# Resident convolution weights, other PSUM banks and an earlier start of the scan inputs in a two-layer attention, Mamba and mixture-of-experts kernel

## The chip, the cores and the metric

The kernel runs on one core of a Trainium2 chip. The core has five engines with an instruction queue each, which run in parallel and meet at semaphores: PE (TensorE, matrix products and transposes, into the eight banks of PSUM), DVE (VectorE), ACT (ScalarE, functions through tables that have to be loaded), POOL (GpSimd) and SP, which here only issues DMAs. Every engine works through its own queue in order: an instruction that waits holds back all that stand behind it. The metric is the time of one execution on the device in microseconds (us); less is better.

## The reference

Everything is float32, for 4 sequences (batches) of 1024 tokens with 128 features. Two layers, each with a mixer and a mixture of experts; shift, scale and gate of each come from a small product with a condition vector:

```python
h = _layernorm(x) * (1 + ca) + sa;  x = x + ga * _L0_attn_ref(h, Wq, Wk, Wv, Wo)
h = _layernorm(x) * (1 + cb) + sb;  x = x + gb * _L0_ffn_ref(h, gate_w, w1, w2)
h = _layernorm(x) * (1 + ca) + sa;  x = x + ga * _L1_attn_ref(h, W_in, conv_w, ...)   # layer 1's own mod
h = _layernorm(x) * (1 + cb) + sb;  x = x + gb * _L1_ffn_ref(h, router_w, w1, w2, bias)
```

- Attention of layer 0: 16 query heads of 64, 4 key/value heads, rotary embedding, causal softmax.
- Experts of layer 0: 8 experts with a hidden width of 176; each token goes to its two best by softmax, `silu(g) * u @ w2`.
- The mixer of layer 1 is a Mamba selective scan: `x, z = split(x @ W_in)`; a causal convolution over 4 tokens and silu; from its result B, C (16 states each) and `delta = softplus(...)`; then `h = exp(delta * A) * h + delta * B * u`, `y = sum(h * C)` over 1024 tokens for 128 x 16 states, plus `u * D`, times `silu(z)`, times `W_out`.
- Experts of layer 1: 8 experts of width 512 with a capacity of 512 tokens each, gelu, the two best of each token; tokens over the capacity are dropped.

## The kernel before, in words

The kernel is written with tiles and pools. A scheduler puts each engine's instructions in order by priority and dependencies, so the order of an engine follows the program only loosely; by hand are only the pairs of matmuls that are kept next to each other (`next_to`, line 197) and a few transfers that are issued after others. A pool's memory is given to later tiles when it is closed, and these wait for the last reader.

**Start.** The condition products run and the first features are normed. SP's queue then issues, in order: the attention weights (`wq` first, line 481 onwards), 44 DMAs that fill the slots of the experts in HBM with zeros (line 491), and the DMAs `rot_v` that swap halves for the rotary embedding (lines 508 and 509). `gate_wT` is loaded from ACT's queue.

**Attention.** Stages (b, c): a batch and a half of its heads. Each stage takes eight blocks of queries in the order 7, 0, 6, 1, 5, 2, 4, 3; `probabilities` makes the scores (`sc`, PE), the masked row extremes (DVE), the exponential (ACT) and the division (POOL); `turned` transposes them, `weighted` multiplies by v, `attend` by `wo`. Beside it run the layer-0 experts of the batch before: `sort_tokens` (line 331) finds each token's place and scatters rows to HBM (`blocks_in`), `Blocks` (lines 393 to 455) runs 23 blocks of 128 rows each (`turn` transposes three blocks, `first` makes `pf`, `second` the result `fye`), and `first_returns` (line 311) gathers the results (`fy`, POOL) and adds them to x (DVE, line 278). Batch 3's experts don't fit in and run beside the scans.

**Scans.** For each batch, `scan_inputs` (line 840) makes from the normed x the convolution (four products of `hT` with `conv_in`, into `p`), xc and sz (Silu on ACT), delta (`pd`, and the softplus in small steps on DVE with Exp on ACT), `dg` (DVE), dt, du (POOL, line 882), and bb and cc. Then come 16 steps m (NCH is 16), 8 for either half of the tokens, each with two of the 16 channel groups. A step is `scan` (line 898): two matmuls `pu` (PE, a bank each), two products with bb (DVE, line 911), two `da` (ACT), two scans `h` (DVE, line 915) and two products `hc` (POOL, line 919). `collected` gathers four hc into the bank `py`, `scan_output` multiplies by sz and W_out (`pw`) and adds to x. That makes 16 pairs and 32 scans for each batch, 64 pairs in all, numbered here by scans from 0 to 127.

Beside the steps run generators, written in the loop at lines 1189 to 1254. `Beside(steps, at, n)` means: from step m = at, n steps of the generator after each m, and the rest after the batch. In the list `beside` they are taken in order after each m, in `among` also between the scan and its gathers. Before the change: in batch 0 `first_returns(2)`, `sort_tokens(3)`, `shift_and_scale`; in batch 1 `first_blocks(3)`; in batch 2 `first_returns(3)`; in each, `dispatch` of the batch before (line 941: the norm, the routing and 16 scatters `slots_in`), and, last in the list, the `scan_inputs` of the next batch from m = 2 (5 in batch 2).

**The end.** `dispatch_last`, 16 calls of `expert` with 512 rows, `last_experts` for the last tokens in blocks of 128, and `collect`, which gathers and stores.

PSUM in layer 1, eight banks: `pu0` to `pu3` for the scans, `py`, `g` for the blocks, `m` for the inputs and the sort, `d` for dispatch, `pw` and every second block.

Of the kernel before, what the change touches and what calls it, by code (L numbers as in the profile page):

```python
# [18 lines left out]
P = 128  # L19
# [5 lines left out]
NEG = -1e30  # L25
LN_EPS = 1e-5
NE = 8
# [22 lines left out]
def adaln_two_layers(ctx: ExitStack, tc: tile.TileContext, I: dict, out: bass.AP):  # L50
# [11 lines left out]
    def load(pool, name, eng=nc.sync):  # L62
# [10 lines left out]
    causal = cst.tile([P, P], F32, name="causal")  # L73
    nc.gpsimd.memset(causal, 0.0)
    nc.gpsimd.affine_select(
        out=causal, in_=causal, compare_op=ALU.is_ge, fill=NEG, base=0, pattern=[[-1, P]], channel_multiplier=1
    )
# [127 lines left out]
    def top2_steps(logits, pool):  # L205
# [5 lines left out]
        def t2(tag):  # L211
            return pool.tile([P, TB], F32, tag=f"r_{tag}", name=f"r_{tag}")[:, :nt]

        def t3(tag):
            return pool.tile([P, TB, NE], F32, tag=f"r_{tag}", name=f"r_{tag}")[:, :nt]
# [43 lines left out]
    f_gate = load(keep, "gate_wT", nc.scalar)  # L259
    loads = []  # L260
# [70 lines left out]
    def sort_tokens(b, kept, pool, ps, tag, xtag="fxn"):  # L331
# [5 lines left out]
        yield from feature_steps(xn, hT, ps, modT[0][:, 4, b : b + 1], modT[0][:, 3, b : b + 1])  # L337
        pl = ps.tile([P, TB, NE], F32, tag="m", name="fpl")
# [8 lines left out]
        pin = ps.tile([P, TB + 1, NE], F32, tag="m", name="fpin")  # L347
# [45 lines left out]
    class Blocks:  # L393
# [9 lines left out]
        def load(self, n):  # L403
            rows_in = f_in[self.b].rearrange("(q p) d -> p q d", p=P)
            m = min(3, NB - 3 * n)
            self.xe = self.pool.tile([P, 3, D], F32, tag="fxe", name="fxe")
            nc.sync.dma_start(self.xe[:, :m], rows_in[:, 3 * n : 3 * n + m])
# [54 lines left out]
    QG = 32  # L462
    with ExitStack() as es:
# [19 lines left out]
        for j in range(4):  # L483
            rows = slice(j * QG, (j + 1) * QG)
            nc.gpsimd.tensor_copy(mask[rows, MW - QG :], causal[rows, rows])

# [174 lines left out]
        for at, (b, c) in enumerate(stages):  # L661
# [7 lines left out]
            back = first_returns(b - 2, ab, 3) if c == 1 and b > 1 else iter(())  # L669
# [45 lines left out]
    m_in = load(w1l, "m_in")  # L715
    m_cb = load(w1l, "m_cb")
    m_B = load(w1l, "m_B")
    m_C = load(w1l, "m_C")
    m_dt = load(w1l, "m_dt")
# [17 lines left out]
    with ExitStack() as es:  # L737
# [12 lines left out]
        conv_in = mc.tile([P, 4, D], F32, name="conv_in")  # L750
        nc.sync.dma_start(conv_in.rearrange("p k d -> p (k d)"), I["m_cwT"].to_broadcast([P, 4 * D]))
        nc.vector.tensor_mul(conv_in, conv_in, m_in[:, :D].unsqueeze(1).to_broadcast([P, 4, D]))

# [20 lines left out]
        def first_blocks(b):  # L774

            blocks = Blocks(b, fb, (ps_g, "g"), [(ps_g, "g"), (ps_m, "d")], rest)
# [63 lines left out]
        def scan_inputs(b):  # L840
# [12 lines left out]
            for tok in halves():  # L853
# [5 lines left out]
                mm(nc, p2, m_in[:, D:], hT[:, tok.start + 3 : tok.stop + 3])  # L859
# [38 lines left out]
        def scan(pair, g, carry, dt, du, bb, cc):  # L898
# [4 lines left out]
            for _ in pair:  # L903
                pus.append(ps_u.tile([P, 512], F32, tag=f"pu{next(turn) % 4}", name="pu"))
            for n in range(2):
# [3 lines left out]
                next_to(n == 0, lambda: mm(nc, pus[n], lhsT, du[rows, tok]))  # L909
# [187 lines left out]
        def last_experts():  # L1097
# [16 lines left out]
            def hidden(j):  # L1114
# [13 lines left out]
                ph = [ps_u.tile([P, NFC, P], F32, tag=f"pu{(j + r) % 4}", name="gph") for r in range(n)]  # L1128
# [59 lines left out]
        output = None  # L1188
        for b in range(B):
            sz, xc, *scanned = inputs.rest()  # L1190
            carry = mb.tile([P, NCH], F32, tag="carry", name="carry")
            beside, among = [], []
            if b == 0:
                beside.append(Beside(first_returns(B - 2, db, 6), 4, 1))
                beside.append(Beside(sort_tokens(B - 1, kept, db, ps_m, "hT2", "hx"), 2, 4))
                beside.append(Beside(shift_and_scale(), NCH - 3, 1))
            if b == 1:
                among.append(Beside(first_blocks(B - 1), 1, 1))
            if b == 2:
                beside.append(Beside(first_returns(B - 1, db, 6), 0, 2))  # L1200
            if sending is not None:
                beside.append(sending)
            if b + 1 < B:
                inputs = Beside(scan_inputs(b + 1), 5 if b == 2 else 2, 3 if b == 2 else 2)
                beside.append(inputs)
            hcs, late = [], None
            for m in range(NCH):
# [22 lines left out]
                if n == NCH // 2 - 1:  # L1230
# [5 lines left out]
                    hcs = []  # L1236
# [180 lines left out]
```

## Time and profile before

| | us |
|---|---|
| median of 3 runs | 2197.03 |
| the three runs | 2189.51, 2197.03, 2200.22 |
| the profiled execution | 2186.78 |
| its span | 2185.1 |
| first scores of attention | 93.44 |
| last `pw` of attention ends | 1424.7 |
| first `pu` | 1470.87 |
| scans of batches 0, 1, 2, 3 | 1471 to 1556, 1588 to 1686, 1686 to 1816, 1851 to 1934 |

The times in a profile count from the start of the span. The page gives each engine's busy time, and the granted clock of TensorE in 40 slices (9 is full). A line of a timeline has the start and the duration in us, the engine, the line of the kernel, the operation, output<-inputs, shapes, the count (on PE an fp32 matmul is more than one record), and in brackets the idle time before it and what released it. SPq and ACTq are DMA issues on those queues. A row of the table by stage has the stretch, its length, the busy time of PE, of PE's weight loads, DVE, ACT and POOL with their counts, the granted clock, and the DMA share and rate.

### The profile page before, as it was taken

How to read it: one execution, taken by the hardware profiler on the slowest of the kernel's cores; microseconds unless marked ns; L12 is line 12 of the kernel's file. 1: busy time of each engine (PE TensorE's matmuls, PEld its weight loads, DVE VectorE, ACT ScalarE, POOL GpSimd, SP SyncE). 2: the span in 40 equal slices, each digit the busy share in tenths (PEclk: the TensorE clock that was granted, in tenths of full speed). 3: DMA queues.
4: the chain of work that ended last, by engine and by line, in shares of the span. 5: the costliest groups of instructions: out<-in, count | busy, mean ns of one | idle time of the engine just before them, and what ended most of it. 6: DMA issues, size and time to landing. Idle time of an engine off the chain costs nothing. (4 is left out here: it accounts for less than half of the span.)

```text
span 2185.1 us, 29044 instructions
## 1 busy us (share of the span) xinstructions
PE 1832.8 (84%) x8957; PEld 972.7 (45%) x8957; DVE 1321.1 (60%) x4001; ACT 939.5 (43%) x2067; POOL 993.6 (45%) x1277
## 2 busy tenths in 40 slices
PE   5399999998999898999988999959698858859784
PEld 3144444454555354455444456523245423227563
DVE  5446566565667755667675566537587785861323
ACT  1145454653454464445374455433564334323221
POOL 1334444346333736523644633244563666571524
PEclk9699999999999998999999999965687757559897
DMA  6300101002222101222200212110121220012425
GB/s 224 126 1 20 30 1 38 12 19 55 72 64 76 48 1 44 77 66 64 77 6 29 69 58 75 35 34 0 35 71 51 75 99 20 1 51 82 131 72 153
DMA packets 103756, 123.59 MB, mean 57 GB/s; under 512 B 15024, under 2 KB 68656, under 8 KB 103600
## 3 DMA queue, kind: packets, MB, share of 16 engines
q1 hardware_dynamic: 84256, 99.01, 15.4%
q0 software_dynamic: 8192, 16.74, 2.5%
q10 hardware_dynamic: 11152, 5.97, 0.9%
q8 instruction: 71, 1.16, 0.2%
q14 instruction: 85, 0.70, 0.1%
HBM read 67.85 MB, written 32.90 MB: 46 GB/s over the span
## 5 line engine op out<-in xcount | busy, mean ns | idle before, releaser
L586 POOL TENSOR_SCALAR pr<-pr,den 128x32 f32<-128x32 f32 (+31 forms) x512 | 353.2, 705 | 301.9 <-DVE den L583 295.8
L580 ACT ACTIVATE pr<-pr,nb 128x32 f32<-128x32 f32 (+31 forms) x512 | 371.6, 727 | 196.9 <-DVE nb L567 193.6
L595 PE MATMUL pt<-ident,pr 128*128 128x128 f32 x2304 | 341.9, 283 | 47.6 <-POOL pr L586 38.1
L46 PE MATMUL sc<-k,q 64*128 64x512 f32 (+14 forms) x1536 | 329.4, 520 | 43.8 <-DVE nb L567 25.3
L595 PEld LDWEIGHTS pt<-ident,pr 128*128 128x128 f32 x2304 | 253.2, 142 | 243.6 <-POOL pr L586 77.4
L46 PE MATMUL po<-pT,v 128*64 128x512 f32 x1152 | 344.7, 621 | 1.8 <-DVE pT L599 1.8
L597 ACT COPY pT<-pt 128x512 f32<-128x512 f32 x288 | 167.7, 582 | 354.9 <-PE pt L595 301.9
L567 DVE CUSTOM_DVE_ANT_0 pr<-sc,mask 128x512 f32<-128x512 f32 (+15 forms) x512 | 272.9, 559 | 73.5 <-PE sc L46 63.9
L599 DVE COPY pT<-pt 128x512 f32<-128x512 f32 x288 | 198.3, 688 | 167.2 <-PE pt L595 154.1
L919 POOL TENSOR_TENSOR hc<-h,cc 128x512 f32<-128x512 f32 x128 | 161.0, 1272 | 127.7 <-DVE h L915 60.2
L46 PEld LDWEIGHTS sc<-k,q 64*128 64x128 f32 x1536 | 122.4, 191 | 198.7 <-DVE nb L567 93.7
L46 PE MATMUL pu<-du,spread 32*128 32x512 f32 x256 | 146.5, 953 | 34.0 <-DVE h L915 30.1
L684 POOL MEMSET pr<- 128x288 f32 x128 | 42.3, 339 | 264.4 <-PE pt L595 260.3
L567 DVE CUSTOM_DVE_ANT_0 pr<-sc,mask,nb 128x416 f32<-128x416 f32 (+15 forms) x256 | 119.9, 496 | 7.0 <-PE sc L46 5.8
L913 ACT ACTIVATE da<-dt,negA 128x512 f32<-128x512 f32 x128 | 91.0, 718 | 75.8 <-DVE h L915 75.5
L911 DVE TENSOR_TENSOR pu<-pu,bb 128x512 f32<-128x512 f32 x128 | 85.9, 686 | 39.9 <-PE pu L46 39.4
L1302 POOL DMA_INDIRECT y<-slots_out,slot x56 | 57.9, 1033 | 108.4 <-PE ph L46 50.7
L46 PEld LDWEIGHTS po<-pT,v 128*64 128x64 f32 x1152 | 69.3, 135 | 84.1 <-issue 42.0
L503 DVE TENSOR_TENSOR rot_w<-proj,sin_sb 128x512 f32<-128x512 f32 x80 | 55.0, 688 | 77.5 <-PE proj L46 44.4
L46 PEld LDWEIGHTS pf<-fxT,fw 128*128 128x128 f32 x552 | 73.5, 202 | 53.6 <-DVE fye L450 15.5
L580 ACT ACTIVATION_READ_ACCUMULATOR pr<-pr,nb 128x1 f32 x512 | 96.3, 188 | 0.0
L545 POOL TENSOR_TENSOR q<-rot_u,rot_v 128x512 f32<-128x512 f32 x64 | 81.3, 1271 | 32.8 <-DMA rot_v<-rot_w 29.1
(273 smaller groups left out, 2714.3 us busy)
## 6 DMA issues: line engine op xcount, KB each, us to landing
fw<-in_f_w SPq DMA_DIRECT2D x92, 320.0 KB, 3.0
rot_v<-rot_w SPq DMA_DIRECT2D x320, 64.0 KB, 2.0
gw<-in_g_w SPq DMA_DIRECT2D x15, 512.0 KB, 5.2
fxe<-blocks_in SPq DMA_DIRECT2D x28, 192.0 KB, 2.6
blocks_out<-fye SPq DMA_DIRECT2D x28, 192.0 KB, 3.0
blocks_in<-mask SPq DMA_DIRECT2D x20, 256.0 KB, 5.2
slots_in<-mask SPq DMA_DIRECT2D x16, 256.0 KB, 4.7
g_w<-in_g_w SPq DMA_DIRECT2D x8, 512.0 KB, 6.4
```

What stands on the lines that cost most here:

```text
L46: return nc.tensor.matmul(out, lhsT, rhs, start=start, stop=stop)
L545: nc.gpsimd.tensor_add(to, u.rearrange("p (n q) -> p n q", q=QG), v.rearrange("p (n q) -> p n q", q=QG))
L567: nc.vector.tensor_tensor_reduce(out=pr[hp][:, g, lo:hi], in0=sc[:, hp, : hi - lo], in1=mask[:, MW - hi + lo :] if hi == nk else mask[:, : ...
L580: nc.scalar.activation(p, p, AF.Exp, bias=nb[:, last, hp : hp + 1], scale=-1.0, accum_out=den[:, hp : hp + 1])
L586: nc.gpsimd.tensor_scalar(p, p, den[:, hp : hp + 1], 1.0, ALU.mult, ALU.mult)
L595: next_to(hp == 0 and g == 0, lambda: nc.tensor.transpose(to, p, ident))
L597: nc.scalar.copy(pT[:, hp, :], pt)
L599: nc.vector.tensor_copy(pT[:, hp, :], pt)
L911: nc.vector.tensor_mul(pu, pu, bb[:, tok])
L913: nc.scalar.activation(da, dt[:, tok], AF.Exp, scale=negA[:, c : c + 1])
L919: nc.gpsimd.tensor_mul(hcs[-1], h, cc[:, tok])
L1302: nc.gpsimd.indirect_dma_start(out=y, out_offset=None, in_=yd[k][:, :], in_offset=bass.IndirectOffsetOnAxis(ap=slot[:, k, t : t + 1], axis=0),
```

## The change

Four parts, all in one diff.

1. The convolution product `conv_in`, `m_cb`, `m_B`, `m_C`, `m_dt` and the second half of `m_in` (as `m_gate`) are loaded right after `gate_wT`, on ACT's queue, and stay for the whole kernel; the first half of `m_in` lies in a pool `cw` that is closed after the product. Their loads after attention go.
2. The room for that: the causal mask has 32 columns instead of 128 (the attention mask is copied once, not four times), the router's tiles `r_` and `fxe` have one buffer, and the returns in attention two buffers `fy` instead of three.
3. PSUM: three banks for `pu` instead of four, and two banks `g0`, `g1` for the blocks; `sort_tokens(3)` uses the bank `d` instead of `m`; the last experts take their banks from one ring. The second matmul of a pair is issued first.
4. Beside the scans: the next batch's inputs are first in the list, from m = 0 (1 in batch 2) with three steps each; `sort_tokens(3)` starts at m = 0; `first_blocks(3)` starts at the end of batch 0 and ends in batch 1, at m = 10; `first_returns(3)` follows there.

```diff
+    m_cb = load(keep, "m_cb", nc.scalar)
+    m_B = load(keep, "m_B", nc.scalar)
+    m_C = load(keep, "m_C", nc.scalar)
+    m_dt = load(keep, "m_dt", nc.scalar)
+    m_gate = keep.tile([P, D], F32, name="m_gate")
+    nc.scalar.dma_start(m_gate, I["m_in"][:, D:])
+
+    conv_in = keep.tile([P, 4, D], F32, name="conv_in")
+    with tc.tile_pool(name="cw", bufs=1) as cw:
+        m_x = cw.tile([P, 1, D], F32, name="m_x")
+        nc.scalar.dma_start(m_x[:, 0, :], I["m_in"][:, :D])
+        nc.scalar.dma_start(conv_in.rearrange("p k d -> p (k d)"), I["m_cwT"].to_broadcast([P, 4 * D]))
+        nc.vector.tensor_mul(conv_in, conv_in, m_x.to_broadcast([P, 4, D]))
...
-            self.xe = self.pool.tile([P, 3, D], F32, tag="fxe", name="fxe")
+            self.xe = self.pool.tile([P, 3, D], F32, tag="fxe", bufs=1, name="fxe")
...
-            back = first_returns(b - 2, ab, 3) if c == 1 and b > 1 else iter(())
+            back = first_returns(b - 2, ab, 2) if c == 1 and b > 1 else iter(())
...
-    m_in = load(w1l, "m_in")
-    m_cb = load(w1l, "m_cb")
-    m_B = load(w1l, "m_B")
-    m_C = load(w1l, "m_C")
-    m_dt = load(w1l, "m_dt")
...
-        conv_in = mc.tile([P, 4, D], F32, name="conv_in")
-        nc.sync.dma_start(conv_in.rearrange("p k d -> p (k d)"), I["m_cwT"].to_broadcast([P, 4 * D]))
-        nc.vector.tensor_mul(conv_in, conv_in, m_in[:, :D].unsqueeze(1).to_broadcast([P, 4, D]))
...
-            blocks = Blocks(b, fb, (ps_g, "g"), [(ps_g, "g"), (ps_m, "d")], rest)
+            blocks = Blocks(b, fb, (ps_g, "g0"), [(ps_g, "g0"), (ps_g, "g1")], rest)
...
-                pus.append(ps_u.tile([P, 512], F32, tag=f"pu{next(turn) % 4}", name="pu"))
-            for n in range(2):
+                pus.append(ps_u.tile([P, 512], F32, tag=f"pu{next(turn) % 3}", name="pu"))
+
+            for n in (1, 0):
                 c = pair[n]
                 rows = slice(32 * (c // 4), 32 * (c // 4) + 32)
                 lhsT = spread[rows, c % 4].rearrange("p a n -> p (a n)")
-                next_to(n == 0, lambda: mm(nc, pus[n], lhsT, du[rows, tok]))
+                next_to(n == 1, lambda: mm(nc, pus[n], lhsT, du[rows, tok]))
...
+        among = []
         for b in range(B):
             sz, xc, *scanned = inputs.rest()
             carry = mb.tile([P, NCH], F32, tag="carry", name="carry")
-            beside, among = [], []
+            beside = []
             if b == 0:
                 beside.append(Beside(first_returns(B - 2, db, 6), 4, 1))
-                beside.append(Beside(sort_tokens(B - 1, kept, db, ps_m, "hT2", "hx"), 2, 4))
+                beside.append(Beside(sort_tokens(B - 1, kept, db, ps_m, "hT2", "hx", "d"), 0, 4))
                 beside.append(Beside(shift_and_scale(), NCH - 3, 1))
+                among.append(Beside(first_blocks(B - 1), NCH - 4, 1))
             if b == 1:
-                among.append(Beside(first_blocks(B - 1), 1, 1))
-            if b == 2:
-                beside.append(Beside(first_returns(B - 1, db, 6), 0, 2))
+                among[0].at = 0
+                beside.append(Beside(first_returns(B - 1, db, 6), NCH // 2 + 2, 2))
             if sending is not None:
                 beside.append(sending)
             if b + 1 < B:
-                inputs = Beside(scan_inputs(b + 1), 5 if b == 2 else 2, 3 if b == 2 else 2)
-                beside.append(inputs)
+                inputs = Beside(scan_inputs(b + 1), 1 if b == 2 else 0, 3)
+                beside.insert(0, inputs)
...
+                if b == 1 and m == NCH // 2 + 2:
+                    among.pop().rest()
...
-            for f in beside + among:
+            for f in beside:
                 f.rest()
...
-        banks = itertools.cycle([(ps_u, "pu0"), (ps_u, "pu1"), (ps_u, "pu2"), (ps_u, "pu3")])
-        outs = itertools.cycle([(ps_y, "py"), (ps_g, "g")])
+        banks = itertools.cycle([(ps_u, "pu0"), (ps_u, "pu1"), (ps_u, "pu2"), (ps_g, "g1")])
+        outs = itertools.cycle([(ps_y, "py"), (ps_g, "g0")])
```

Left out are the mask of 32 columns, `bufs=1` of the router's tiles, the argument `bank` of `sort_tokens`, `m_gate` in the product of sz, and the last experts' banks from `next(banks)`. In the new order of DVE, taken from the built program, dg of the next batch stands behind scans 26, 49 and 88; before, behind 32, 62 and 96.

## The prediction

> **What bounds the kernel now.** I read the page first (busy shares and the slices), then a table of busy time by stage, the stage edges taken from the scan instructions, then the timelines of the engines at each edge.
>
> The page: nearly three quarters of the span is attention, with PE busy and at full clock; after it come slices with PE at 5 to 9 tenths and the clock at 5 to 8.
> ```profile
> span 2185.1 us, 29044 instructions
> PE 1832.8 (84%) x8957; PEld 972.7 (45%) x8957; DVE 1321.1 (60%) x4001; ACT 939.5 (43%) x2067; POOL 993.6 (45%) x1277
> PEclk9699999999999998999999999965687757559897
> ```
> Busy time by stage (PE, weight loads, DVE, ACT, POOL, then granted clock): start, attention, its end, then scan 0, a gap, scan 1, scan 2, a gap, scan 3, the last experts. The last row is part of scan 0.
> ```profile
> 0.00:100.00 100.00, 41.84 (x118) 23.59 (x120) 43.17 (x135) 12.86 (x23) 18.54 (x78) 0.80 0.58 191
> 100.00:1425.00 1325.00, 1223.39 (x6593) 645.83 (x6589) 840.21 (x2844) 662.43 (x1557) 587.89 (x850) 0.98 0.15 43
> 1425.00:1471.00 46.00, 22.56 (x46) 9.56 (x46) 16.49 (x78) 17.66 (x31) 21.92 (x30) 0.65 0.14 40
> 1471.00:1556.00 85.00, 80.12 (x204) 29.73 (x204) 67.05 (x109) 37.32 (x68) 46.12 (x38) 0.59 0.05 17
> 1556.00:1588.00 32.00, 17.15 (x47) 7.24 (x48) 9.39 (x57) 14.46 (x24) 14.27 (x15) 0.58 0.05 18
> 1588.00:1686.00 98.00, 88.69 (x382) 47.16 (x381) 78.91 (x157) 48.65 (x94) 47.76 (x42) 0.78 0.23 67
> 1686.00:1816.00 130.00, 94.21 (x290) 40.79 (x290) 103.01 (x199) 47.84 (x97) 84.17 (x72) 0.67 0.22 73
> 1816.00:1851.00 35.00, 25.83 (x118) 14.06 (x116) 12.76 (x64) 15.32 (x27) 23.39 (x21) 0.83 0.08 29
> 1851.00:1934.00 83.00, 64.98 (x161) 21.25 (x160) 72.52 (x116) 30.15 (x59) 56.11 (x47) 0.56 0.03 9
> ...
> 1471.00:1500.00 29.00, 29.00 (x73) 10.82 (x76) 20.84 (x25) 13.99 (x34) 13.67 (x11) 0.50 0.00 1
> ```
> Attention is PE's (1223 of 1325). The scans are not one engine's: scan 0 is PE's (80 of 85, at a clock of 0.59), scan 2 DVE's and POOL's, and in two stretches of 32 and 35 us no scan runs: the inputs of the next batch are still in the making. Both start as PE ends attention: PE waits 14.87 us for a weight product, and at the second gap 9.55 us for a step of the softplus, a chain of short operations over ACT and DVE.
> ```profile
> 1438.80 0.68 DVE L752 TENSOR_TENSOR conv_in<-conv_in,m_in_sb 128x512 f32<-128x512 f32 x1
> ...
> 1439.59 6.51 PE L46 MATMUL p<-hT,conv_in 128*128 128x512 f32 x8 [14.87 <-DVE conv_in L752]
> ...
> 1577.21 2.05 PE L46 MATMUL p<-dg,ones 128*128 128x512 f32 x2 [9.55 <-DVE ln_r L159]
> ```
> The start is SP's, whose DMA issues stand one behind the other from 28.71 to 90.5, and the first scores come 3 us later:
> ```profile
> 28.71 0.34 SPq L64 DMA_DIRECT2D wq_sb<-in_wq  x1
> ...
> 31.53 18.33 SPq L491 DMA_DIRECT2D blocks_in<-mask  x24
> ...
> 63.57 0.62 SPq L508 DMA_DIRECT2D rot_v<-rot_w  x1
> ...
> 93.44 5.82 PE L46 MATMUL sc<-k,q 64*128 64x512 f32 x16 [13.28 <-POOL q L545]
> ```
> And a pair of scans with nothing beside it, in scan 0, takes 3.87 us from scan to scan:
> ```profile
> 1485.62 2.32 DVE L915 TENSOR_TENSOR_SCAN h<-da,pu 128x512 f32<-128x512 f32 x2
> 1487.86 0.68 DVE L911 TENSOR_TENSOR pu<-pu,bb 128x512 f32<-128x512 f32 x1
> 1488.88 0.70 DVE L911 TENSOR_TENSOR pu<-pu,bb 128x512 f32<-128x512 f32 x1 [0.35 <-PE pu L46]
> 1489.49 2.32 DVE L915 TENSOR_TENSOR_SCAN h<-da,pu 128x512 f32<-128x512 f32 x2
> ```
>
> **The change part by part.** All sums are against the profiled execution: 2186.8 us with a span of 2185.1. It lies 10.2 under the median of the three runs (2197.0), below the lowest (2189.5).
>
> *Weights loaded at the start: +9.* Seven more DMAs are issued on ACT's queue behind gate_wT (28.65), at some 0.45 each (rows of 0.36 to 0.43 and the steps between issues), so 3.2 us. ACT's two table loads (1.28 each) and the Ln and Exp of the second norm stand behind them: Exp ends at 35.4 instead of 34.5. The pool in which m_x lies is freed and given to wq, so wq's load must wait until the conv_in product has read m_x, and in DVE's order that product stands behind three rows xn of the second norm. These started at 35.36; with ACT 0.9 to 1.2 later and three rows of 0.27, the product (0.68) ends near 37.6. SP issues wq then, not at 28.71, and behind it in the queue stand five weights, 44 zero fills (31.8 us) and the first rot_v: the whole chain up to the first scores moves by 9. Attention is PE's from there, so nothing takes it back. Bounds: 0 (the product lands elsewhere in time) and 11.
>
> The smaller mask product, the one-buffer router tiles, fxe with one buffer (its load of 2.6 us is issued a turn of some 17 us ahead) and fy with two (POOL's gathers of 1.26 then go at the pace of DVE's adds, beside PE's work) I cost at nothing, covered by attention's PE; without that cover, fxe costs its 2.6 at each of 8 turns of three batches.
>
> *Conv starts at once: -8.* conv_in and its load leave the end of attention, where the product stood on DVE behind x<-fy (1434.64 waits 3.06 for a gather). PE can begin at 1424.7 instead of 1439.6, 14.9 sooner. The rest of the chain to the first pu at 1470.87 is not shorter: xc, sz, pd, the softplus, dg, dt, du (2.35). Next late is ACT, whose Silu, Ln and Exp change tables at 1.28 each while the norms of the returns and the sort share it; in the new order the sort of batch 3 (fpl 3.58, tp 2.2 and about 16 us of DVE) also comes ahead of dg. I walk that to a first pu at 1463. Bounds: 0 and 14.9; the middle, for want of a row that decides.
>
> *Inputs first, and the sort out of scan 0: -22 and -8.* In the new order dg stands behind scans 26, 49 and 88 instead of 32, 62 and 96, so both gaps lose their cause. Their work does not vanish: 17.15 us of PE in the first. Scan 0 has PE busy 80.1 of 85, so PE's floor for scan 0 and gap is 80 + 17 = 97 less some 10 for the sort (fpl, tp, and fpin of about 4), 87 against 117 now. So 30 us, of which I give 22 to the inputs and 8 to the sort. Bounds: 0 (each wait comes back inside) and 33 with the sort free.
>
> *The second gap: -22.* Scan 2 and gap hold 165 us with PE busy 120, DVE 116, POOL 108. Moving the inputs in front gains at most 45 by PE; 35 is the gap itself. But dg then waits in DVE's order among scans, and du (2.35) with the scatters in POOL's, so I take two thirds of the gap, as in the first. Bounds 0 and 35.
>
> *Returns and scatters: -8.* Before, 16 gathers (1751 to 1775, 1.26 each) stop the scans: five start between 1749.8 and 1784.3, and DVE idles 2.83 us at 1757 for one transfer. Now the last blocks end by scan 54 (before, 80) and the returns lie at scans 56 to 64, in the same pairs as 16 scatters. POOL then has 32 x 1.27 and ten hc x 1.27, 53 us for five pairs; before, the two stretches took 33 (1695 to 1728) and 35 (1750 to 1785), 68 for 14 scans. Fourteen scans need about 27 us in any case (3.87 a pair) and five pairs 19, so 41 us are lost before and 34 after: -8, bounded by -41 (all of it beside other work) and +15 (a row of gathers that stops the scans at both ends, twice the 8). This is the term I trust least.
>
> *Three banks for pu: +18.* With three, the second tile of a pair uses the bank of the first tile of the pair before, so PE starts the two matmuls when that scan ends. The cycle is a product of 0.61, one more, a scan of 1.21, then 2.08 for the matmuls (the two run side by side) and some 0.2 for the hand-overs: 4.7 against 3.87, +0.83 for a pair that nothing else fills. Scans and products take 243 of DVE's 361 us from 1460 to 1960, and the other 118 are spread unevenly; I count 22 of 64 pairs as empty, mostly in scans 0 and 3. Bounds: 0 (all filled) and 64 x 1.8 = 115, if the gather py (1.94 in every second pair) stands in the way too.
>
> The clock decides the size: while PE was busy 29.0 of 29.0 us (1471 to 1500) it stayed at 0.50. The Trainium skill, "TensorE: Matmul & The Clock Gate" (What's actually happening), says that activity releases the throttle after some 3.4 us; this row does not agree. By that rule the matmuls would take half of 2.08, a pair 3.7, and the ring would cost nothing: the sum would be 18 lower. The same page (A second HAM failure mode) speaks against the change: a matmul stream that waits on cycling PSUM idles often enough to lose the clock; stretches at 0.78 would then fall to 0.5.
>
> *Dispatch, blocks and last experts in their own banks: 0.* The block matmuls (138 first pf, 24.5 us) and pw no longer share "d", and the last experts still draw on four banks. Bounds -5 (a wait of pw of 3.68 at 1565 gone) and +5.
>
> The sum: 9 - 8 - 22 - 8 - 22 - 8 + 18 = -41, so 2146 for an execution such as the profiled one and 2156 by the median. I say 2151.
>
> **The rivals.** *The gaps close in full.* PE's 80 of 85 in scan 0 speaks against it, the idle DVE (67 of 85) for it. Then -33 - 35 - 8 - 8 - 8 + 9 = -83, with the ring filled by the inputs: 2104 to 2114.
>
> *The work only moves.* The scans take what the gaps gave, since PE at 0.5 and the shared bank m pace them: for it speaks scan 0, at 80 of 85; against it scan 2, with 36 us of idle PE. The gaps then give 10 each, not 22: 2170 and 2180 by the two bases; with no gain in returns 2178 to 2195, little or no change.
>
> *The ring decides (slower).* One mechanism: each pair's matmuls wait for the scan before and PE's gathers stand between, at half clock. The gains without the ring are 59, so it decides from 0.92 us per pair over 64 pairs. At 0.83 it costs 53, about no change; with py's half of 1.94 in each, 1.8, at three quarters of the pairs 86: +27, so 2214 to 2224. For it: scan 0 has PE without idle time at 0.5. Against it: new work fills the waits.
>
> **How the numbers follow.** The forecast (2125 to 2175) 0.52; gaps closed in full (under 2125) 0.13; work only moved (2175 to 2208) 0.20; ring (over 2208) 0.15. Half a per cent, 11 us, is what a measurement of this kernel can tell from no change, so faster means under 2186 and slower over 2208. Half of the third case is still faster: faster 0.75, same 0.10, slower 0.15. The range leaves out the far half of the full gain and most of the ring's case: 2108 to 2210.
>
> **What would show it.** wq issued near 37.7 and the first scores near 102; no wait of PE for conv_in at the end of attention and a first pu some 38 after its last pw, not 46; no stretch of 10 us without a scan at batch edges; in quiet pairs 4.7 us from scan to scan with pu waiting on DVE h; a thick stretch of POOL near scans 54 to 64. The prediction is wrong if the scan stage, 463 us now, does not come out at 410 to 430, or if the ring's waits exceed 0.9 us in most pairs.

## The result and the profile after

The changed kernel takes 2209.73 us (median of 7 runs, 2205.56 to 2215.85), the kernel before 2197.90 in as many runs beside it (2189.51 to 2201.18). The ratio is 1.0062, with a 95% interval of 1.0038 to 1.0085: slower by 12 us by the medians and 0.6% by the ratio, where 41 us less was forecast. The time lies 0.3 us inside the upper end of the range, on the other side of no change.

The profiles of both kernels, cut at the same events (first scores, last `pw` of attention, first `pu`, first and last scan, first expert product `ph`), give the account. The last column is the forecast of the same stretch.

| stretch, us | before | changed | difference | forecast |
|---|---|---|---|---|
| start to first scores | 93.4 | 103.2 | +9.7 | +9 |
| first scores to end of the last pw | 1331.3 | 1332.8 | +1.5 | 0 |
| last pw to first pu | 46.1 | 53.9 | +7.8 | -8 |
| first pu to first scan | 2.9 | 3.5 | +0.6 | 0 |
| first scan to end of the last | 459.9 | 448.5 | -11.4 | -42 |
| last scan to first ph | 32.6 | 38.3 | +5.7 | 0 |
| first ph to end | 218.8 | 229.6 | +10.8 | 0 |

The last row is not put down to the change: e4 below, which is the changed kernel but for one tile at the start, takes 216.9 us for this stretch, and over four groups of four runs it takes 217 to 221 us in three and 235 to 238 in the other, with nearly the same instructions. The profile of the kernel before is also of a quick execution, 2186.78 us, below all seven beside the changed kernel. The rows above the last add up to 13.9 us, 0.64%, close to the measured 0.62%. Against the forecast of -41 that is 55 us: 31 in the scans, 16 ahead of the first pu, 6 behind the last scan, and 3 in the other rows.

The start went as the forecast had it. From the timelines of DVE, SP and PE, changed kernel:
```profile
36.98 0.68 DVE L275 TENSOR_TENSOR conv_in<-conv_in,m_x 128x512 f32<-128x512 f32 x1
...
37.80 0.34 SPq L65 DMA_DIRECT2D wq_sb<-in_wq  x1
...
40.55 19.29 SPq L504 DMA_DIRECT2D blocks_in<-mask  x24
...
103.18 6.17 PE L47 MATMUL sc<-k,q 64*128 64x512 f32 x16 [11.58 <-POOL q L558]
```
wq leaves 0.14 us after the product has ended, at 37.8 (forecast 37.7); ahead of it SP waits 7.5 us for this product.

The end of attention did not. PE begins the convolution 0.38 us after its last pw, with no wait for `conv_in`; but look at ACT (its timeline, and two rows of PE's):
```profile
1450.35 1.28 ACT L156 ACT_TABLE_LOAD   x1
1462.23 0.21 ACT L156 ACTIVATE ln_r<-ln_ve 128x8 f32<-128x8 f32 x1 [10.60 <-DVE ln_ve L154]
...
1465.13 1.28 ACT L861 ACT_TABLE_LOAD   x1
1466.43 0.69 ACT L861 ACTIVATE xc<-p,m_cb_sb 128x512 f32<-128x512 f32 x1
...
1464.40 1.25 PE L186 MATMUL tp<-ident,fxn 128*128 128x128 f32 x3 [12.17 <-ACT fxn L175]
...
1489.82 2.08 PE L47 MATMUL pu<-du,spread 32*128 32x512 f32 x4
```
The second xc, which the first scan needs, stands in ACT's queue behind the logarithm of another norm, and that waits 10.6 us for statistics on DVE, which stand behind returns whose gathers POOL issues one by one. So it comes 30.5 us after the last pw (27.7 before), although the convolution begins 14.5 us sooner after it. The other part of the delay comes behind it: from the second xc to the first pu it takes 23.4 us, 18.4 before. There the sort has put its wait for `fpl` into DVE's queue ahead of dg:
```profile
1480.48 0.22 DVE L225 TENSOR_REDUCE r_m<-fpl 128x8 f32<-128x64 f32 x1 [2.76 <-PE fpl L47]
1480.62 1.22 DVE L877 TENSOR_TENSOR dg<-ident,sp_d 128x1024 f32<-128x1024 f32 x1
```

The stages of the scans, one row a batch, by the table by stage (PE, weight loads, DVE, ACT, POOL, clock):
```profile
1493.30:1589.40 96.10, 81.00 (x249) 31.74 (x247) 74.68 (x117) 48.74 (x86) 60.09 (x53) 0.66 0.13 40
1589.40:1733.80 144.40, 94.16 (x479) 52.24 (x482) 109.30 (x242) 54.72 (x108) 83.32 (x75) 0.77 0.31 97
1733.80:1846.00 112.20, 82.57 (x246) 32.39 (x246) 77.57 (x162) 55.60 (x96) 62.96 (x50) 0.65 0.02 8
1846.00:1941.80 95.80, 66.73 (x198) 24.88 (x198) 73.25 (x130) 35.25 (x69) 63.31 (x52) 0.52 0.03 10
```
Cut in the same way (from a batch's first scan to the next one's, gaps included), before took 114, 105, 157 and 83 us. The gaps are gone: the longest time from the start of one scan to the next, 36.8 us before, is 11.4, and the time without a scan at the three batch edges falls from 72.8 to 9.6 us in all. Yet no engine is busy over 85% in any batch. The pairs themselves have grown: without those edges a pair takes 6.9 us on average, 6.0 before. In a quiet stretch of batch 3 (DVE's timeline):
```profile
1878.10 2.33 DVE L920 TENSOR_TENSOR_SCAN h<-da,pu 128x512 f32<-128x512 f32 x2
1881.48 1.30 DVE L916 TENSOR_TENSOR pu<-pu,bb 128x512 f32<-128x512 f32 x2 [1.05 <-PE pu L47]
1882.91 2.33 DVE L920 TENSOR_TENSOR_SCAN h<-da,pu 128x512 f32<-128x512 f32 x2
1887.02 1.30 DVE L916 TENSOR_TENSOR pu<-pu,bb 128x512 f32<-128x512 f32 x2 [1.78 <-PE pu L47]
```
That is 4.81 us from scan to scan, forecast 4.7; the next pair, behind another wait for pu, takes longer still.

### The profile page after: what moved, and what is told of

The parts are those of the page before. It is cut to its first block, busy times and chain, and to the rows that moved or that the text cites. A ratio compares the mean times of both kernels' runs of the same rounds, so it can differ in the third digit from the quotient of the medians.

```text
span 2209.7 us, 29061 instructions
## 1 busy us (share of the span) xinstructions
PE 1809.1 (82%) x8957; PEld 971.4 (44%) x8957; DVE 1323.7 (60%) x4001; ACT 950.3 (43%) x2075; POOL 994.5 (45%) x1277
## 4 chain that ended last, share of the span: by engine, by line
PE 48%; issue 20%; DVE 10%; POOL 6%; ACT 6%; DMA 5%; SPq 2%; another core or an unknown queue 0%; ACTq 0%; POOLq 0%; DVEq 0%
PE po L47 12%; PE pt L608 11%; PE sc L47 6%; ACT pr L593 4%; PE pf L47 4%; DVE pr L580 3%; POOL pr L599 3%; PE ph L47 3%; PE pw L47 3%; PE ypy L47 2%; PE proj L47 2%; PE p L47 1%; DMA blocks_in<-fxn,f_placei 1%; DVE h L920 1%; DMA fy<-blocks_out,f_placei 1%
## 5 line engine op out<-in xcount | busy, mean ns | idle before, releaser
L612 DVE COPY pT<-pt 128x512 f32<-128x512 f32 x288 | 198.2, 688 | 167.8 <-PE pt L608 157.4
L47 PE MATMUL pu<-du,spread 32*128 32x512 f32 x256 | 108.4, 936 | 55.6 <-DVE h L920 40.7
```

The source lines that it names most:

```text
L47: return nc.tensor.matmul(out, lhsT, rhs, start=start, stop=stop)
L612: nc.vector.tensor_copy(pT[:, hp, :], pt)
```

## The experiments

Each run is compared with the kernel before on its own chip. The four groups (e, f, g, h) were run apart, so ratios are compared between them, and stretches of the profile up to the first ph, in us. Each stretch is of one profiled execution; the two of the same kernel, f1 and h3, agree to 0.6 us in every column.

| run | ratio (95% interval) | first scores | last pw to pu | scans | last scan to ph |
|---|---|---|---|---|---|
| e1_four_pu_banks | 1.0117 (1.0082 to 1.0152) | 102.6 | 51.2 | 457.4 | 40.2 |
| e2_three_pu_banks | 0.9935 (0.9908 to 0.9962) | 93.7 | 47.6 | 440.7 | 31.7 |
| e3_late_weights | 0.9999 (0.9980 to 1.0017) | 93.8 | 60.3 | 444.2 | 38.0 |
| e4_wq_free | 1.0029 (1.0014 to 1.0044) | 97.1 | 54.0 | 447.8 | 38.2 |
| f1_sort_on_d | 0.9904 (0.9877 to 0.9930) | 93.6 | 46.3 | 425.3 | 39.4 |
| f2_ring_alone | 0.9984 (0.9968 to 1.0000) | 93.1 | 45.9 | 454.6 | 31.7 |
| f3_banks_inputs_first | 1.0053 (1.0030 to 1.0077) | 94.1 | 66.0 | 431.9 | 38.3 |
| f4_banks_blocks_early | 0.9982 (0.9968 to 0.9995) | 93.1 | 47.8 | 451.0 | 31.8 |
| g1_inputs_from_2 | 0.9987 (0.9972 to 1.0002) | 102.8 | 51.4 | 437.8 | 31.7 |
| g2_sort_on_d_mid_weights | 0.9923 (0.9900 to 0.9947) | 93.1 | 52.6 | 421.3 | 39.3 |
| g3_sort_on_d_inputs_listed_first | 0.9912 (0.9885 to 0.9940) | 93.4 | 47.8 | 425.4 | 39.6 |
| g4_four_banks_sort_on_d | 0.9911 (0.9879 to 0.9943) | 93.4 | 58.1 | 417.1 | 39.8 |
| h1_four_banks_inputs_from_2 | 0.9947 (0.9928 to 0.9966) | 93.4 | 55.5 | 429.3 | 39.1 |
| h2_four_banks_mid_weights | 0.9949 (0.9928 to 0.9969) | 93.6 | 48.9 | 434.5 | 39.3 |
| h3_sort_on_d_again | 0.9877 (0.9849 to 0.9904) | 93.7 | 46.3 | 425.9 | 39.4 |
| h4_sort_on_d_ring | 0.9897 (0.9866 to 0.9928) | 93.4 | 47.9 | 434.0 | 31.8 |

The scans of some of them by batch (from its first scan to the next batch's), with the time without a scan at the three edges, and the rest divided by the 64 pairs:

| us | before | changed | e2 | e3 | f1 | g4 | h1 | h4 |
|---|---|---|---|---|---|---|---|---|
| batch 0 | 114.2 | 96.1 | 89.3 | 92.8 | 90.7 | 79.8 | 88.6 | 86.2 |
| batch 1 | 105.4 | 144.4 | 131.6 | 142.8 | 118.3 | 114.0 | 140.4 | 125.4 |
| batch 2 | 157.4 | 112.2 | 128.1 | 112.7 | 130.2 | 125.5 | 114.1 | 130.7 |
| batch 3 | 82.8 | 95.8 | 91.7 | 95.9 | 86.0 | 97.9 | 86.2 | 91.8 |
| edges | 72.8 | 9.6 | 19.0 | 11.3 | 58.3 | 5.2 | 84.9 | 24.1 |
| a pair without edges | 6.0 | 6.9 | 6.6 | 6.8 | 5.7 | 6.4 | 5.4 | 6.4 |

The last column of the first table has two values. In all runs with 31.7 to 32.6 us one of the two selections of the last batch's `dispatch` (`r_s<-r_s,r_z` on DVE) stands behind the last scan, in all with 38 us or more both do: the 7 us are the same work, among the scans or behind them.

### The banks, first pass

Two theories after the result: the ring of three banks eats the gain (A), or the work of the gaps only moved (B). The PSUM part was taken out of the change (e1), and put alone into the kernel before (e2):

```diff
# e1, against the changed kernel
+            blocks = Blocks(b, fb, (ps_g, "g"), [(ps_g, "g"), (ps_m, "d")], rest)
+                pus.append(ps_u.tile([P, 512], F32, tag=f"pu{next(turn) % 4}", name="pu"))
+            for n in range(2):
+                beside.append(Beside(sort_tokens(B - 1, kept, db, ps_m, "hT2", "hx"), 0, 4))   # bank m
# e2, against the kernel before: the same places as in the change
```

> The changed kernel with its PSUM part taken back: four banks for pu, the blocks on g and d, the sort on m, the last experts' banks by number, the first matmul of a pair first. Theory A (three banks for pu hold the matmuls back to the scan before, so that every detour of PE stops the scans): the time from the first to the last scan falls from 447 us to about 400 to 410, the total to 2160 to 2175. Theory B (the work of the gaps only moved, PE and POOL pace the scans with any number of banks): the scans stay at 440 to 450 us and the total within 10 us of 2210. Of the tail after the last scan, 268 us now and 251 before, some 8 come back if the ring of the last experts made them late.

> The kernel before with the PSUM part of the change alone, in the old schedule. Theory A: the scans, 459 us from first to last, take 20 to 50 us longer, the total is 2215 to 2245. Theory B: the scans stay within 8 us, the total within 10 us of 2197, apart from up to 8 us in the tail after the last scan.

Both went against A: without the PSUM part the changed kernel is slower (1.0117), with it alone the kernel before is faster by 0.65%. In e1 batches 0, 1 and 3 are 14, 36 and 8 us shorter than in the changed kernel and batch 2 is 67 longer: with the sort back on m the returns of batch 3 lie there, and no scan starts for 58.8 us. B, as it was put for e2, fell too, since e2 is no standstill. The part holds several edits, so it was split, with four banks for the first and with only the ring in the second:

```diff
# f1 (and h3): the sort of batch 3 on d
-                beside.append(Beside(sort_tokens(B - 1, kept, db, ps_m, "hT2", "hx"), 2, 4))
+                beside.append(Beside(sort_tokens(B - 1, kept, db, ps_m, "hT2", "hx", "d"), 2, 4))
# f2: the ring alone
-                pus.append(ps_u.tile([P, 512], F32, tag=f"pu{next(turn) % 4}", name="pu"))
-            for n in range(2):
+                pus.append(ps_u.tile([P, 512], F32, tag=f"pu{next(turn) % 3}", name="pu"))
+            for n in (1, 0):
```

> The kernel before with one edit: the sort of batch 3 uses the bank d instead of m, which the inputs of the next batch use; four banks for pu, old schedule. Theory C (the gain of the PSUM part is that the sort no longer holds up the inputs at the bank m): the gap of 34 us after the first 32 scans goes below 10, the scans take some 20 us less, the total is 15 to 25 us under the kernel before. Theory D (it is the order and number of the pu banks): the gap stays, the total within 6 us of the kernel before.

> The kernel before with three banks for pu and the second matmul of a pair first, all else as before (sort on m, blocks on g and d). Theory C: the gap of 34 us stays and the quiet pairs take 0.5 to 0.8 us longer, 10 to 20 us more in all. Theory D: the total falls by 10 to 16 us and the gap shrinks.

One argument of one call takes 1.0% off (1.2% when it was run again), and no kernel here is clearly faster: the scans fall from 460 to 425 us, of which 7 come back behind the last scan (39.4 against 32.6). Theory C had the size right, not the way: the gap halves (34 to 17 us), it does not close. PE's timeline of f1 shows where the sort went, and with it the inputs of batch 1:
```profile
1462.99 1.84 PE L46 MATMUL fpl<-gate_wT_sb,fhT 128*128 128x8 f32 x16
...
1478.99 0.57 PE L46 MATMUL fpin<-f_mine,ones 128*128 128x8 f32 x2
...
1481.40 2.08 PE L46 MATMUL pu<-du,spread 32*128 32x512 f32 x4
...
1515.34 3.70 PE L46 MATMUL p<-hT,conv_in 128*128 128x512 f32 x8
```
In the kernel before, the timeline of PE has them inside the scans:
```profile
1495.67 3.58 PE L46 MATMUL fpl<-gate_wT_sb,fhT 128*128 128x8 f32 x16
...
1523.42 0.57 PE L46 MATMUL fpin<-f_mine,ones 128*128 128x8 f32 x2
...
1539.50 6.07 PE L46 MATMUL p<-hT,conv_in 128*128 128x512 f32 x8
```
In a bank that dispatch and the blocks don't use yet, the sort's products all run in PE's waits at the end of attention, at no cost there (the first pu comes 46.3 us after the last pw, before 46.1); its scatters follow from 1483 to 1538 us, before from 1536 to 1588. Batch 1's convolution starts 34 us after the first pu instead of 69. The blocks start sooner too, since they need the sort (first `fye` at scan 32 instead of 41), and batch 2, where their returns lay, goes from 157 to 130 us, while batch 1, which now has more of the blocks, goes from 105 to 118. f2 shows no loss from three banks in the old schedule, only 0.16% of gain whose interval touches none.

### The ring again

e1 had put the sort back onto m, so it took away a gain together with a loss. g4 takes the new schedule with four banks and the sort on d (weights late), to stand beside e3; h4 puts the ring into the kernel with the sort on d, to stand beside f1 and h3.

```diff
# e3, against the changed kernel: the weights are loaded after attention as before
# g4, against e3
-            blocks = Blocks(b, fb, (ps_g, "g0"), [(ps_g, "g0"), (ps_g, "g1")], rest)
+            blocks = Blocks(b, fb, (ps_g, "g"), [(ps_g, "g"), (ps_m, "d")], rest)
-                pus.append(ps_u.tile([P, 512], F32, tag=f"pu{next(turn) % 3}", name="pu"))
-            for n in (1, 0):
+                pus.append(ps_u.tile([P, 512], F32, tag=f"pu{next(turn) % 4}", name="pu"))
+            for n in range(2):
# h4, against f1: "% 3" and "for n in (1, 0)", nothing else
```

> The changed kernel with the convolution weights loaded after attention again, all else as changed. If the load of wq behind the convolution product is what moved the start, the first scores are back near 93.5 instead of 103.2. The end of attention then waits again for the weights. If the early weights gained nothing there (ACT paces the first inputs), the first scan comes as long after the last pw as in the changed kernel, 57 us, and the total is 2197 to 2203; if they gained what the forecast said, 8 us, the total is 2205 to 2211.

> The changed kernel with the weights loaded late (0.9999 of the kernel before) and four banks for pu, the blocks on g and d, the sort kept on d: the new schedule without the ring of three. If the ring is what makes the pairs of the new schedule long, the scans fall from 444 to 420 to 430 us and the total is 0.990 to 0.995. If the schedule itself does (inputs, blocks and dispatch of several batches in the same pairs), the scans stay above 438 and the total is 0.996 to 1.003.

> The sort on d in the old schedule, with three banks for pu and the second matmul first; the blocks stay on g and d. If the ring costs its 0.4 to 0.8 us a pair wherever the inputs are not held up elsewhere, the scans take 435 to 445 us instead of 425 and the total is 0.993 to 0.997. If the ring costs nothing in the old schedule, the total is 0.988 to 0.992, and what the whole PSUM part lost against the sort alone was the blocks' banks.

(g4 also puts the last experts' banks back, behind the scans.) e3 to g4: the ratio falls from 0.9999 to 0.9911, 19 us, and the scans from 444.2 to 417.1, 27.1 us. The waits of the scans, e3 (engine, line, what it waited for; total us, times, longest):
```profile
DVE pu L912 <- PE pu L47: 43.0, 30, 6.4
PE pu L47 <- DVE h L916: 42.4, 24, 8.6
PE py L47 <- POOL hc L920: 50.9, 22, 10.9
```
and g4:
```profile
DVE pu L912 <- PE pu L47: 16.0, 13, 3.6
PE pu L47 <- DVE h L916: 19.5, 6, 7.6
PE py L47 <- POOL hc L920: 20.8, 7, 6.5
```
DVE waits 27.0 us less for PE, and the scans are 27.1 shorter, but by batch the two are not the same us. In batch 0 they fit: 13.0 us shorter, with 12.4 less of this wait (16.5 to 4.1), which is what a PE that is a pair ahead would give. Batch 1 is 28.8 us shorter with only 1.6 less of it; there PE's waits for the scan and for hc go, 21.7 and 20.9 us in e3 and none in g4. Batches 2 and 3 are 12.8 and 2.0 longer. g4 also has the blocks' second bank back on d, where they end later (last `fye` at scan 64 instead of 54), so that their returns move from batch 1 to batch 2. So the 27 us are the ring's and that edit's together, and how they divide was not measured in this schedule.

h4 has the ring alone, in the old schedule: the scans 434.0 against 425.3 and 425.9, 8 us, of which 7.6 come back between the last scan and the first ph (31.8 against 39.4), where one selection has moved among the scans. From the first scan to the first ph the ring costs 0.5 to 1.1 us there. Its ratio, 0.9897, lies between the two of the sort alone. That is the second case of its expectation: what the whole PSUM part (e2) lacks against the sort alone lies in the other bank edits. In e2, with the blocks on g0 and g1, the scans take 6.7 us more than in h4; the intervals of the two ratios overlap.

### The schedule

f3 and f4 add halves of the new schedule to the whole PSUM part (e2), g1 takes the inputs' start back to m = 2 (5 in batch 2) and their steps to two in batches 0 and 1 in the changed kernel, g3 only lists the inputs first on top of the sort on d:

```diff
# f3: inputs first, from m = 0
+                inputs = Beside(scan_inputs(b + 1), 1 if b == 2 else 0, 3)
+                beside.insert(0, inputs)
# f4: the lines of the change on first_blocks, first_returns and among
# g1, against the changed kernel
-                inputs = Beside(scan_inputs(b + 1), 1 if b == 2 else 0, 3)
+                inputs = Beside(scan_inputs(b + 1), 5 if b == 2 else 2, 3 if b == 2 else 2)
# g3, against f1
-                beside.append(inputs)
+                beside.insert(0, inputs)
```

> The kernel before with the whole PSUM part (which alone gained 16 us) and, of the schedule, only the inputs of the next batch first and from m = 0 with three steps. If early inputs pay, the long waits between scans (17, 12 and 16 us are left with the PSUM part alone) go, and the total is 10 to 20 us under that of the PSUM part, 0.98 to 0.985 of the kernel before. If their steps only delay the scans of the same batch, it is within 6 us of it, 0.991 to 0.997.

> The kernel before with the whole PSUM part and, of the schedule, only the last blocks from the end of batch 0 and their returns in batch 1. If crowding the blocks, the returns and the dispatch into batch 1 is what the changed kernel pays, this is 10 to 20 us slower than the PSUM part alone, near the kernel before (0.998 to 1.003). If the early returns free the scans of batch 2, as the forecast had it, it is 5 to 10 us faster, 0.989 to 0.991.

> The changed kernel with the inputs of the next batch still first in the list, but from m = 2 (5 in batch 2, with two steps in the others) as before the change. If inputs from m = 0 crowd the end of attention (work of batch 1 that ACT and DVE take ahead of batch 0's own inputs), the first pu comes 46 to 48 us after the last pw instead of 54 and the total is 6 to 12 us under the changed kernel, 0.999 to 1.003 of the kernel before. If not, it stays near 54 us and the total within 4 us of the changed kernel, 1.004 to 1.009.

> The kernel before with the sort on d and the inputs of the next batch first in the list, with the old starts and steps. If only the place in the list holds dg back to the end of a batch, the three waits of 17, 18 and 27 us between batches that the sort on d leaves go, and the total is 0.980 to 0.987 of the kernel before. If the pairs take the work up as longer pairs, it is 0.988 to 0.995.

f3 reads batch 3's x for the inputs before all returns are added to it; the instructions are the same, the values are not. That is also why the change moves the blocks: inputs that early need returns that are earlier still. f3 closes the gaps as theory has it (431.9 us of scans, 440.7 in e2), and loses 18 us before the first pu (66.0 against 47.6) and 7 before the first ph. f4 loses 10 us of scans: 26 in batch 1 (158 us, 132 in e2), where blocks, returns and dispatch now meet, against 15 won in batch 2. g1 wins 2.4 us before the first pu, 10.7 in the scans and 6.6 before ph. g3 is the sort on d and nothing more: the order in the list does not matter.

h1 is the new schedule with four banks, sort on d, late weights, and inputs from m = 2 (g4 with g1's line).

> The changed kernel's schedule with late weights, four banks for pu, the sort on d, the blocks on g and d, and the inputs first in the list but from m = 2 (5 in batch 2). If inputs from m = 0 are what puts the first pu 58 us after the last pw (46 with the sort on d alone), it is 47 to 52 here; the scans take 410 to 420 us, and the total is 0.983 to 0.989 of the kernel before, 3 to 12 us under the sort on d alone. If the new schedule has nothing left to gain, it is within 4 us of the sort on d alone.

On one chip it takes 0.9947 and the sort on d alone 0.9877: the new schedule in this form costs 15 us. The first pu is not back at 47 to 52 as expected but at 55.5: the second xc is as early as in f1 (25.6 and 26.2 us after the last pw), but the sort, which starts at m = 0 here, puts a wait of 3.8 us for `fpin` between the softplus steps on DVE, and du comes 53.1 us after the last pw instead of 43.7. The scans take 429.3, not 410 to 420, and h1 is no test of closed gaps: 47 us pass without a scan ahead of batch 2 and 28 ahead of batch 3. g4, from m = 0, has shorter scans (417.1) and pays for them before the first pu (58.1).

The line of the edges in the table above settles theory B. With four banks, the time without a scan at the edges is 84.9 us in h1, 58.3 in f1 and 5.2 in g4, and the pairs take 5.4, 5.7 and 6.4: of 80 us closed from h1 to g4, 12 are left in the scans. Most of the work of the gaps did move into the pairs.

### The weights

e4 keeps the early loads, but puts m_x where no other tile waits for it; g2 and h2 load the weights on SP in the second stage of attention, on top of f1 and h1.

```diff
# e4, against the changed kernel
-    with tc.tile_pool(name="cw", bufs=1) as cw:
-        m_x = cw.tile([P, 1, D], F32, name="m_x")
-        nc.scalar.dma_start(m_x[:, 0, :], I["m_in"][:, :D])
+    hT0 = keep.tile([P, S + 3], F32, name="hT0")
+    m_x = hT0[:, 3 : 3 + D]
+    nc.scalar.dma_start(m_x, I["m_in"][:, :D])
# g2 and h2: the same loads on nc.sync, called at the head of the second stage
+            if at == 1:
+                conv_weights()
```

> The changed kernel with m_x in a tile that attention leaves unused (hT0) instead of memory that is given to wq; the same loads and products. If wq's wait for the convolution product is the whole cost at the start, wq is issued near 28.7, the first scores come at 93.5 to 95 instead of 103.2 and the total is 2199 to 2202. If the seven DMA issues on ACT are the cost, the first scores stay above 100.

> The kernel before with the sort on d (0.990 alone) and the convolution weights resident, but loaded on SP's queue at the second stage of attention and multiplied through a tile that attention leaves unused, so that the start is untouched; with the smaller tiles of the change. If PE's wait of 15 us for the product at the end of attention is worth what the forecast gave it, the first pu comes 6 to 10 us sooner after the last pw than 46, the total is 0.986 to 0.988. If the sort fills that wait anyway, the gain is under 4 us, 0.988 to 0.992.

> The same with the convolution weights resident, loaded on SP's queue in the second stage of attention. Late weights cost 6 us in the changed kernel, where work of the next batch fills the wait; if that holds here, the total is 4 to 8 us under the run with late weights, 0.980 to 0.986; if the sort fills the wait, as it did with the old schedule, within 3 us of it.

In e4 (SP's and PE's timelines) wq leaves at once:
```profile
28.26 0.34 SPq L65 DMA_DIRECT2D wq_sb<-in_wq  x1
...
31.96 0.33 SPq L65 DMA_DIRECT2D cos_sb<-in_cos  x1
...
34.86 18.98 SPq L503 DMA_DIRECT2D blocks_in<-mask  x24
...
97.10 4.62 PE L47 MATMUL sc<-k,q 64*128 64x512 f32 x12 [13.17 <-POOL q L557]
```
6.1 of the 9.7 us come back. For the rest, SP pauses ahead of cos and of sin, and the zero fills start 3.3 us later than in the kernel before. By SP's waits in the trace, it waits 2.4 us there for wq's load and 1.7 for that of `m_C`; why these two hold it is not shown. At the other end, early weights bring the first pu forward by 6.4 us (e3 60.3, changed kernel 53.9; h1 55.5, h2 48.9). With the sort on d in the old schedule they bring nothing: g2's first pu is later (52.6), although the convolution begins 0.4 us after the last pw: a logarithm again stands ahead of the second xc, which comes 26.0 us after the last pw, in f1 26.2, and then DVE waits 2.9 us for the sort's `fpl` between two steps of the softplus. Its ratio is 0.9923 against 0.9904 and 0.9877. In h2 the scans give back 5 us, so it equals h1.

## Why the prediction was wrong, by its own steps

The forecast was on the wrong side in two terms above all: the order ahead of the first pu, and the belief that pairs with other work in them take up more work, and the ring's waits, at a small price.

- *Weights at the start, +9:* right in place and size (+9.7; wq at 37.8). e4 shows m_x's memory to be two thirds of it.
- *Conv starts at once, -8: failed, +7.8.* The mechanism holds (-6.4 from e3 to the changed kernel), but the prediction took the order ahead of the first pu as given otherwise. It noted that ACT is next late and that the sort comes ahead of dg, and still walked it to 8 us sooner. Two things hold the pu back. Inputs from m = 0 put a further norm into ACT's queue, which was not counted: in all six runs with them (changed kernel, e1, e3, e4, f3, g4) a logarithm ahead of the second xc waits 8.0 to 10.7 us for DVE; in the others none waits over 5. That its norm is batch 2's is argued from the returns it follows. And the sort's products put DVE's waits for them amid the softplus and dg: 2.8 us for `fpl` in the changed kernel, 2.9 in g1 and g2, 3.8 for `fpin` in h1. In the schedule of e2 the early inputs alone cost 18 us there (f3), against the -8; in the changed kernel only 2.4 come back without them (g1), and g2 has nothing from early weights without them.
- *Inputs first, sort out of scan 0: -22 and -8.* The gap closed, as the forecast had it, and the floor for scan 0 and its gap, 87 us of PE, was a fair estimate: from the first pu to batch 1's first scan g4 takes 82.7 us, the changed kernel with its ring 99.6 (in both a part of the work, the sort's above all, now stands ahead of the first pu).
- *The second gap, -22, with the returns, -8:* the gap closed, the time did not go. Batches 1 and 2 together, where these 30 us were to come from, take 256.6 us instead of 262.8, 6 less (23 less in g4). The thick stretch of returns and scatters came as described (53 us for five pairs): nine scans at the end of batch 1 take 52.3 us, POOL is busy 42.5 of them and PE 14:
```profile
1681.50:1733.80 52.30, 14.03 (x40) 2.79 (x44) 32.41 (x52) 7.22 (x10) 42.52 (x41) 0.50 0.33 118
```
  f4, with the move alone, has scans that are 10 us longer where 8 less were booked. And batch 3, for which nothing but the ring was booked, takes 13 us more (15 in g4, without the ring). The step that failed is to take two thirds of a gap as gain because engines are idle in the pairs: the pair is a chain through PE, DVE, ACT and POOL, and with no engine busy over 85% of a batch the pairs still grew by 0.8 us.
- *The sort:* booked as part of the second term and at 8 us for the room it leaves on PE. It was the change's one large gain, 35 us of scans, 28 from the first scan to the first ph, since in the bank m, which it shared with the inputs, it stood in their way, and the blocks behind it came later. The prediction listed "separate banks" for the dispatch at 0 with bounds of 5 and did not ask who else shares m.
- *Three banks, +18: mis-sized and misplaced.* The cycle of 4.7 us was right (4.81). But the term counted 22 empty pairs, mostly in batches 0 and 3, and let all others hide the ring. From e3 to g4 it is 27, with the blocks' banks, and by batch 13, 29, -13 and -2: most in batch 1, which has the most work beside the scans, and nothing in batch 3. In the old schedule the ring alone costs about 1 us from the first scan to the first ph. With inputs from m = 2 in the new schedule the banks' part is 3 us of scans against h2 and 8 against h1 (g1 437.8).
- *Dispatch at 0:* behind the last scan the changed kernel has both selections of the last dispatch, before one, +5.7, for which the sum has no term.
- *The rivals:* "the ring decides" had the sign and the place, not the cause: its 86 us would have needed 1.8 us a pair, and 27 over 64 pairs are 0.42. It took the ring, the queue ahead of the first scan and the start together, so the right sign there is luck. "The work only moves" comes nearest in the scans, and named the shared bank m, but as what would stay, while the change had taken the sort off it. Its range without a gain in the returns should end at 2188, not 2195 (2197 - 9).
- *A reading:* the wait of 9.55 us at 1577.21, given there for the second gap and the softplus, lies in the first gap, and what ended it is `ln_r`, a step of a norm.

The clock: batch 3 ran at 0.52 in the changed kernel, and from 1485 to 1505 us, where PE was busy 18.6 of 20 us, it was 0.50, so the pu matmuls kept their 2.08 us and the ring its price. The Trainium skill, "TensorE: Matmul & The Clock Gate" (What's actually happening), would have released the throttle after some 3.4 us of activity; that stretch doesn't agree. Its warning of clock lost to cycling PSUM (A second HAM failure mode) is not borne out by these runs either: the scans' granted clock is 0.70 in g4 and 0.68 in e3, and 0.67 and 0.68 in h3 and h4.

## What to carry to other kernels

Two streams that took turns in one PSUM bank held each other back here as an in-order queue would, and one argument of one call was worth 1.0 to 1.2%: before moving work in a schedule, list who shares each bank, and give the stream that others wait for one that is free at that time. Filling a gap is worth only what the loop around it can take up without longer turns; a floor from busy times doesn't tell that, the length of a turn with and without the gaps does. And work that is allowed to start earlier also gets in front of what was on the path: look at what it puts ahead in each in-order queue, at the head of the stage as well as inside it.

## What was not expected of the hardware

- ACT's table load takes 1.28 us and the next instruction starts 0.02 later (1448.83 to 1450.13 in the changed kernel), so in this trace a change of function costs the load and nothing visible beside it. Nine such loads stand between the last pw and the second xc in the changed kernel, 11.5 us, beside the logarithm's wait of 10.6: the order of Ln, Exp and Silu, which asks for the loads, and the wait made ACT late together.
- The stretch from the first ph to the end, with nearly the same instructions, differs by some 18 us between groups of runs (217 to 221 and 235 to 238), more than the effect under study. Why is open. The scans of one kernel in two groups agreed to 0.6 us (425.3 and 425.9).
